# Adding softmax weights of four heads with one VectorE instruction instead of two, in a two-layer attention kernel

## The chip, the cores and the metric

The kernel runs on one core of a Trainium2 chip. The metric is the device time of one execution in microseconds, as the median of some executions. The engines of the core are TensorE (PE in the profile; its weight loads are PEld), VectorE (DVE), ScalarE (ACT), GpSimd (POOL) and SyncE (SP, which here only issues DMAs). Each engine works through its own instructions in order, and semaphores hold an instruction until what it needs is there.

## What is computed

The input is x of shape (4, 256, 64, 64) in fp32: 4 images, 256 channels, 4096 pixels. Two layers follow one another, each with a residual connection and a group normalization (32 groups) ahead of it:

```python
x = x + attention_A(groupnorm(x))   # q: 1x1 convolution; k, v: 2x2 convolution, stride 2; 8 heads of 32
x = x + attention_B(groupnorm(x))   # q, k, v: 1x1; attention in 4 areas; plus a 7x7 depthwise convolution of v; 1x1 projection
# attention: softmax(q k^T / sqrt(32)) v, per head
```

In layer A each of the 4096 queries of an image sees 1024 keys. In layer B the image is cut into 4 areas of 1024 pixels, and a query sees the 1024 keys of its area. So both layers have the same attention work: 4096 queries x 1024 keys x 8 heads an image.

## The kernel before

**Units and steps.** The eight blocks (layer A for four images, then layer B for four images) are cut into units. A unit is one chunk of 512 queries and one half of the heads (4 heads of 32 channels). There are 16 units a block, 128 in all. A unit has 8 steps, one for each tile of 128 keys; so the main loop at the end of `direct_path` makes 1024 steps, numbered by unit g and step j.

**What a step does.** `scores` lets TensorE multiply keys and queries of the four heads (L263); the result is keys by queries, 128x512 for each head, in two PSUM tiles of two heads each. ScalarE takes the exponential of each of the two tiles (L267), a 128x1024 instruction each, and writes the softmax weights p to SBUF. One step later `weighted` multiplies them by the values (L274) and adds up in PSUM over the eight steps. The divisor of the softmax, the sum of p over all keys, is made in two parts: VectorE adds the weights of steps 1 to 7 to those of step 0, element by element (L813, in `sum_up`), and after the last step TensorE multiplies this sum by ones (`divisors`, L283). No maximum is subtracted; the divisors are checked against a limit at the end, and a second program, `general_path`, would run if one were beyond it.

**The tiles p.** The weights of a step lie in two tiles of 128x2x512 fp32 (two heads each) with the tag "p", of which there are 10 buffers. The pair of step 0 is held until the divisors of its unit are made, since the sum is made in it. The chunks of the first image (`first`), one row block at the end (`rb`) and a small tile (`within`) share the tag.

**The order.** The order of instructions on every engine is the order in which the Python code issues them (`manual_schedule`). In each step the code issues the scores, the first exponential, what earlier steps had put off to this one (`later`), the weighted values of the step before, the second exponential, what a plan holds for this step (`plan`, filled by `at(g, j, ...)`), and then parts of side tasks. `soon(n, f)` puts f off by n steps. The additions of a step are put off by one step, the divisors of a unit and what follows them (`divide`) by three.

**What divides.** `divide` copies the divisors out of PSUM (L292), sends them through DRAM so that they lie on 128 partitions (L299, L300, GpSimd's DMA queue), takes reciprocals on VectorE (L306, with a sum for the check in L307), sends them out (L308) and broadcasts them back (L310), and VectorE multiplies the attention result by them (L313). These steps lie in the plan at fixed places of the next two units. Layer A then adds the residual (L436) and takes statistics for the next normalization (L441) on VectorE, and SyncE stores the chunk (L442). Layer B adds the convolution (L573), projects on TensorE (L157, `ops`) and adds bias and residual on VectorE (L588), and SyncE stores the result (L591).

**Side tasks.** Projections to q, k and v, the depthwise convolution as matrix products (L747, with bands and rows that SyncE loads at L728 and L731) and the output projection are side tasks on TensorE. They wait in a queue, `side`, and a step takes none, one, two or three parts of them, by how many wait. All share one PSUM bank (the tag "side"), which must be read out before the next task can write it. The means of the group normalization (L222) need VectorE's aggregate (L217).

Of the kernel before, what the change touches and what calls it, by code (L numbers as in the profile page):

```python
# [9 lines left out]
FP = mybir.dt.float32  # L10
I32 = mybir.dt.int32
AF = mybir.ActivationFunctionType
# [3 lines left out]
P = 128  # L16
B, C, HH, WW = 4, 256, 64, 64
N = HH * WW
CT = C // P
NH, HD = 8, 32  # L20
NAREA = 4
# [3 lines left out]
NKT = MK // P  # L25
CH = 512
NCH = N // CH
# [12 lines left out]
SCALE = HD ** -0.5  # L40
# [15 lines left out]
def direct_path(  # L56
# [19 lines left out]
    V, S, G, T = nc.vector, nc.scalar, nc.gpsimd, nc.tensor  # L76

    const = ctx.enter_context(tc.tile_pool(name="const", bufs=1))
    pool = ctx.enter_context(tc.tile_pool(name="work", bufs=1))
# [25 lines left out]

    first = [pool.tile([P, CT, CH], FP, tag="p", name=f"first_{c}", bufs=10) for c in range(NCH)]
    for c in range(NCH):
        nc.sync.dma_start(first[c], xv[0][:, :, c * CH : (c + 1) * CH])  # L110
    wq0_sb = const.tile([P, CT, C], FP, name="wq0_sb")
# [34 lines left out]
    ones = const.tile([P, HD], FP, name="ones")  # L146
# [12 lines left out]
    def ps_pair(name):  # L159
        return psum.tile([P, 2, CH], FP, tag="s", name=name, bufs=3)  # L160
# [9 lines left out]
    def at(g, j, f):  # L170
        g, j = g + int(j // NKT), int(j % NKT)
        plan.setdefault((g, j), []).append(f)
# [75 lines left out]
    qs, ks, vs, atts, dens, avs = {}, {}, {}, {}, {}, {}  # L248
# [7 lines left out]

    def scores(unit, j):
        q, k = unit[1](), unit[2]()
        p = [pool.tile([P, 2, CH], FP, tag="p", name="p", bufs=10) for _ in range(2)]
        pairs = [ps_pair("s"), ps_pair("s")]  # L260
        for h in range(4):
            rows = slice(HD * h, HD * h + HD)
            T.matmul(  # L263
                pairs[h // 2][:, h % 2, :], lhsT=k[rows, unit[0], j * P : (j + 1) * P], rhs=q[rows, :],
                start=True, stop=True,
            )
        exps = [lambda i=i: S.activation(p[i], pairs[i], AF.Exp, scale=SCALE) for i in range(2)]  # L267
        return p, exps

    def weighted(unit, j, p, av):  # L270

        v = unit[3]()
        for h in range(4):
            T.matmul(  # L274
                av[HD * h : HD * h + HD, :], lhsT=v[:, j, unit[0] * P + HD * h : unit[0] * P + HD * h + HD],
                rhs=p[h // 2][:, h % 2, :], start=(j == 0), stop=(j == NKT - 1),
            )

    def divisors(g, p):

        dens[g] = ps_pair("den")[:, 0, :]
        for h in range(4):
            T.matmul(  # L283
                dens[g][HD * h : HD * h + HD, :], lhsT=ones, rhs=p[h // 2][:, h % 2, :], start=True, stop=True,
            )

    def divide(g, unit):

        den_sb = pool.tile([P, CH], FP, tag="den", name="den_sb", bufs=1)
        few = pool.tile([P, 2, CH // HD], FP, tag="few", name="few", bufs=2)  # L290
        rows = dram.tile([4, CH], FP, tag="rows", name=f"rows_{g}", bufs=4)
        S.copy(den_sb, dens.pop(g))  # L292
        if g == len(units) - 1:
            rb = pool.tile([P, CH], FP, tag="p", name="rb", bufs=10)
            V.reciprocal(rb, den_sb)
            V.tensor_mul(unit[4]()[:, unit[0], :], avs.pop(g), rb)
            spare.extend((den_sb, rb))
            return
        G.dma_start(rows, den_sb[0:P:HD, :])  # L299
        G.dma_start(few[:, 0, :], rows.rearrange("h (q n) -> (h q) n", n=CH // HD))  # L300
        made = {}

        def reciprocals():
            rb = made["rb"] = pool.tile([P, CH], FP, tag="rb", name="rb", bufs=1)
            recs = dram.tile([4, CH], FP, tag="recs", name=f"recs_{g}", bufs=4)
            V.reciprocal(few[:, 1, :], few[:, 0, :])  # L306
            V.tensor_reduce(sums[:, :, g], few, AX.X, ALU.add)  # L307
            G.dma_start(recs.rearrange("h (q n) -> (h q) n", n=CH // HD), few[:, 1, :])  # L308
            for h in range(4):
                G.dma_start(rb[HD * h : HD * h + HD, :], recs[h : h + 1, :].to_broadcast([HD, CH]))  # L310

        def multiply():
            V.tensor_mul(unit[4]()[:, unit[0], :], avs.pop(g), made["rb"])  # L313

        at(g + 1, 7, reciprocals)
        at(g + 2, 4, multiply)
# [459 lines left out]
    units = []  # L776
# [16 lines left out]
    def soon(steps, f):  # L793
        later.setdefault(now[0] + steps, []).append(f)
# [13 lines left out]

    def sum_up(g, j, ps):

        for i in range(2):
            if j:
                soon(1, lambda i=i: V.tensor_add(ps[0][i], ps[0][i], ps[j][i]))  # L813
        if j == NKT - 1:
            soon(3, lambda: divisors(g, ps[0]))
            soon(3, lambda: divide(g, units[g]))
# [3 lines left out]
    while now[0] < last or plan or later or side:  # L820
        g, j = divmod(now[0], NKT)
        if now[0] < last:
            if j == 0:
                ps = {}

            ps[j], exps = scores(units[g], j)
            exps[0]()
        for f in later.pop(now[0], []):
            f()
        if before is not None:  # L830
            weighted(*before)
            if j == 0:
                avs[g - 1] = pool.tile([P, CH], FP, tag="av", name="av_sb", bufs=2)
                S.copy(avs[g - 1], before[3])
# [13 lines left out]
        if now[0] < last:  # L848
            if j == 0:
                av = psum.tile([P, CH], FP, tag="av", name="av", bufs=1)  # L850
            sum_up(g, j, ps)
            before = units[g], j, ps[j], av
        now[0] += 1


    within = pool.tile([P, 2 * len(units)], FP, tag="p", name="within", bufs=10)
    V.tensor_scalar(within, sums.rearrange("p k g -> p (k g)"), LIMIT, None, ALU.is_le)
    least = pool.tile([P, 1], FP, tag="least", name="least", bufs=1)
    V.tensor_reduce(least, within, AX.X, ALU.min)
    ps = ps_pair("count")[0:1, 0, 0:1]  # L860
# [550 lines left out]
def two_attention_layers(tc: tile.TileContext, *args: bass.AP):  # L1411
    nc = tc.nc
    with tc.tile_pool(name="verdict", bufs=1) as pool:
        bad = pool.tile([1, 1], I32, name="bad")
        direct_path(tc, *args, bad)
        count = nc.values_load(
            bad, min_val=0, max_val=P, skip_runtime_bounds_check_because="a count of partitions"
        )
        with tc.If(count > 0):
            general_path(tc, *args)  # L1420
# [39 lines left out]
```

## Time and profile before

| What | Value |
|---|---|
| Median of 3 runs | 3265.79 us (3263.93 to 3267.28) |
| The profiled execution's own time | 3265.73 us |
| Its span, first to last instruction | 3264.0 us |
| TensorE busy (matmul) | 3181.3 us, 97% |
| VectorE busy | 2508.4 us, 77% |
| ScalarE busy | 2524.3 us, 77% |
| GpSimd busy | 493.6 us, 15% |
| Additions L813 on VectorE | 1792, mean 1220 ns |
| Exponentials L267 on ScalarE | 2048, mean 1026 ns |
| Mean granted TensorE clock | 0.989 |

The profile is one execution on the chip. Busy times are unions: where two instructions of one engine overlap, the time counts once. In the table of groups a row gives the source line, the engine, the operation, the tiles written and read, the shape, the count, then the busy time and the mean of one, and last the engine's idle time ahead of these instructions with the one that ended it. The chain that ended last is followed back from the last instruction, at each step to what released it, or to the one before it on its engine. The timeline lists instructions with start, length, engine, line and count; neighbours of one kind are merged into one row, with the time from the start of the first to the end of the last. The ends of matmuls are modelled.

### The profile page before, as it was taken

Reading aid. Unit: us, or ns where it says so; the run is one execution under the profiler, and the core shown is the slowest. Engines: PE = TensorE matmul, PEld = TensorE weight load, DVE = VectorE, ACT = ScalarE, POOL = GpSimd, SP = SyncE. Lnnn points to the kernel's source line nnn. Section 1 sums busy time; section 2 is a strip of 40 time slices with the busy share of each in tenths; the row PEclk is TensorE's granted clock in tenths of the full one; section 3 lists DMA queues with packets and bytes.
Section 4 is the critical chain, followed back from the end, with each engine's and each line's share of the span. In section 5 each row is a group of like instructions: output and inputs, shape, how many; then the busy total and the mean of one; then the engine's idle time right before and its main releaser. Section 6 shows DMA issues by size and latency. Waiting matters only on the chain.

```text
span 3264.0 us, 75650 instructions
## 1 busy us (share of the span) xinstructions
PE 3181.3 (97%) x30754; PEld 963.2 (30%) x30754; DVE 2508.4 (77%) x2717; ACT 2524.3 (77%) x2993; POOL 493.6 (15%) x923
## 2 busy tenths in 40 slices
PE   7999999999999999999999899999999999999997
PEld 4233322233233333223222223232232333222221
DVE  3777896778877777778767577777787788788887
ACT  3888787787887778888867677777777777788775
POOL 0111121111211111111111111111111111111111
PEclk9999999999999999999999999999999999999998
DMA  5243434454444456677766666666554655523212
GB/s 179 44 109 78 109 89 93 96 125 108 114 114 132 122 153 154 173 174 174 187 168 151 164 155 165 174 154 170 135 156 124 156 157 152 135 68 81 65 47 57
DMA packets 648172, 421.50 MB, mean 129 GB/s; under 512 B 411756, under 2 KB 556620, under 8 KB 647816
## 3 DMA queue, kind: packets, MB, share of 16 engines
q1 hardware_dynamic: 619368, 380.11, 46.0%
q0 software_dynamic: 28448, 36.48, 4.6%
q8 instruction: 244, 4.00, 0.5%
q14 instruction: 112, 0.92, 0.1%
HBM read 318.32 MB, written 98.09 MB: 128 GB/s over the span
## 4 chain that ended last, share of the span: by engine, by line
PE 87%; DMA 6%; issue 2%; SPq 2%; DVE 1%; ACT 1%; POOL 0%; DVEq 0%; ACTq 0%; POOLq 0%
PE s L263 31%; PE av L274 27%; PE den L283 4%; DMA rows<-vals 4%; PE ops L157 3%; PE k0ps L157 3%; PE q0ps L157 3%; PE v0ps L157 3%; PE k1ps L157 3%; PE vals_ps L157 3%; PE conv_ps L747 3%; PE q1ps L157 3%; DVE p L813 1%; ACT p L267 1%; SPq L556 1%
## 5 line engine op out<-in xcount | busy, mean ns | idle before, releaser
L813 DVE TENSOR_TENSOR p<-p 128x1024 f32<-128x1024 f32 x1792 | 2111.2, 1220 | 543.6 <-ACT p L267 491.1
L267 ACT ACTIVATE p<-s 128x1024 f32<-128x1024 f32 x2048 | 2016.3, 1026 | 539.0 <-PE s L263 524.3
L263 PE MATMUL s<-q,k_A 32*128 32x512 f32 x4096 | 603.9, 640 | 6.9 <-ACT p L267 6.6
L263 PE MATMUL s<-q,k_B 32*128 32x512 f32 x4096 | 600.1, 646 | 0.3 <-ACT p L267 0.3
L274 PE MATMUL av<-p,v_B 128*32 128x512 f32 x4096 | 550.5, 608 | 0.0
L274 PE MATMUL av<-p,v_A 128*32 128x512 f32 x4096 | 549.7, 604 | 0.0
L310 POOL DMA_DIRECT2D rb<-recs x508 | 252.0, 501 | 451.5 <-DMA recs<-few 367.1
L263 PEld LDWEIGHTS s<-q,k_B 32*128 32x128 f32 x4096 | 166.3, 184 | 386.7 <-issue 297.0
L263 PEld LDWEIGHTS s<-q,k_A 32*128 32x128 f32 x4096 | 173.2, 183 | 338.0 <-issue 253.5
L308 POOL DMA_DIRECT2D recs<-few x127 | 70.0, 551 | 1284.8 <-DVE sums L307 1207.5
L274 PEld LDWEIGHTS av<-p,v_B 128*32 128x32 f32 x4096 | 87.9, 108 | 384.2 <-issue 340.5
L274 PEld LDWEIGHTS av<-p,v_A 128*32 128x32 f32 x4096 | 88.6, 108 | 381.3 <-issue 333.5
L747 PE MATMUL conv_ps<-rows,band 88*32 88x128 f32 x4096 | 139.2, 277 | 28.9 <-DMA rows<-vals 28.9
L747 PEld LDWEIGHTS conv_ps<-rows,band 88*32 88x32 f32 x4096 | 123.8, 139 | 100.6 <-issue 80.3
L157 PE MATMUL ops<-cv,wp_sb 128*32 128x512 f32 x1024 | 136.3, 612 | 9.9 <-issue 6.4
L300 POOL DMA_DIRECT2D few<-rows x127 | 72.3, 569 | 477.5 <-DMA rows<-den_sb 468.0
L283 PE MATMUL den<-p,ones 128*32 128x512 f32 x1024 | 138.7, 604 | 2.2 <-DVE p L813 2.2
L299 POOL DMA_DIRECT2D rows<-den_sb x127 | 74.4, 586 | 436.7 <-ACT den_sb L292 429.9
L157 PE MATMUL k0ps<-taps,wk_sb 128*32 128x256 f32 x2048 | 128.9, 383 | 3.0 <-ACT taps L245 3.0
L157 PE MATMUL q1ps<-h,wqkv_sb 128*32 128x512 f32 x1024 | 131.5, 592 | 0.0
L157 PE MATMUL vals_ps<-hv,wqkv_sb 128*32 128x512 f32 x1024 | 130.2, 594 | 0.0
L157 PE MATMUL k1ps<-h,wqkv_sb 128*32 128x512 f32 x1024 | 128.7, 592 | 0.2 <-ACT cout L758 0.2
(86 smaller groups left out, 1690.8 us busy)
## 6 DMA issues: line engine op xcount, KB each, us to landing
rows<-vals SPq DMA_DIRECT2D x512, 195.9 KB
rb<-recs POOLq DMA_DIRECT2D x508, 64.0 KB, 3.2
band<-mats SPq DMA_DIRECT2D x128, 176.0 KB
vala<-vout SPq DMA_DIRECT2D x128, 144.0 KB
vals<-vout SPq DMA_DIRECT2D x128, 144.0 KB
vc<-vala SPq DMA_DIRECT2D x64, 288.0 KB
hq<-in_x SPq DMA_DIRECT2D x32, 512.0 KB
xc<-in_x SPq DMA_DIRECT2D x32, 512.0 KB
```

Of the source, the lines that this page charges most:

```text
L157: T.matmul(out[cols, :], lhsT=lhsT[:, cols], rhs=rhs, start=start, stop=stop)
L263: T.matmul(pairs[h // 2][:, h % 2, :], lhsT=k[rows, unit[0], j * P : (j + 1) * P], rhs=q[rows, :], start=True, stop=True,)
L267: exps = [lambda i=i: S.activation(p[i], pairs[i], AF.Exp, scale=SCALE) for i in range(2)]
L274: T.matmul(av[HD * h : HD * h + HD, :], lhsT=v[:, j, unit[0] * P + HD * h : unit[0] * P + HD * h + HD], rhs=p[h // 2][:, h % 2, :], start= ...
L283: T.matmul(dens[g][HD * h : HD * h + HD, :], lhsT=ones, rhs=p[h // 2][:, h % 2, :], start=True, stop=True,)
L299: G.dma_start(rows, den_sb[0:P:HD, :])
L300: G.dma_start(few[:, 0, :], rows.rearrange("h (q n) -> (h q) n", n=CH // HD))
L308: G.dma_start(recs.rearrange("h (q n) -> (h q) n", n=CH // HD), few[:, 1, :])
L310: G.dma_start(rb[HD * h : HD * h + HD, :], recs[h : h + 1, :].to_broadcast([HD, CH]))
L556: nc.sync.dma_start(cv[:, t, :].rearrange("p (f r x) -> p r f x", f=TX, r=RC)[:, y - c * RC], conv[b][t * P : (t + 1) * P, r * TX : (r + 1 ...
L747: T.matmul(ps[HD * m : HD * m + HD, (2 * k + i) * size : (2 * k + i + 1) * size].rearrange("p (y x) -> p y x", y=NY), lhsT=band[:, half].r ...
L813: soon(1, lambda i=i: V.tensor_add(ps[0][i], ps[0][i], ps[j][i]))
```

## The change

A step's weights of all four heads lie in one tile of 128x4x512 (128x2048). The tag "p" has 5 buffers of this size instead of 10 of half the size. The two exponentials each write one half of the tile. VectorE adds a step's weights to the sum in one instruction of 128x2048 instead of two of 128x1024, put off by one step as before. The matmuls read the same data from the new tile. The chunks of the first image lie in pairs in such tiles.

```diff
-    first = [pool.tile([P, CT, CH], FP, tag="p", name=f"first_{c}", bufs=10) for c in range(NCH)]
+    first = [pool.tile([P, 2, CT, CH], FP, tag="p", name=f"first_{a}", bufs=5) for a in range(NAREA)]
+    first = [first[c // 2][:, c % 2] for c in range(NCH)]
...
     def scores(unit, j):
         q, k = unit[1](), unit[2]()
-        p = [pool.tile([P, 2, CH], FP, tag="p", name="p", bufs=10) for _ in range(2)]
+        p = pool.tile([P, 4, CH], FP, tag="p", name="p", bufs=5)
...
-        exps = [lambda i=i: S.activation(p[i], pairs[i], AF.Exp, scale=SCALE) for i in range(2)]
+        exps = [lambda i=i: S.activation(p[:, 2 * i : 2 * i + 2], pairs[i], AF.Exp, scale=SCALE) for i in range(2)]
...
-                rhs=p[h // 2][:, h % 2, :], start=(j == 0), stop=(j == NKT - 1),
+                rhs=p[:, h, :], start=(j == 0), stop=(j == NKT - 1),
...
-                dens[g][HD * h : HD * h + HD, :], lhsT=ones, rhs=p[h // 2][:, h % 2, :], start=True, stop=True,
+                dens[g][HD * h : HD * h + HD, :], lhsT=ones, rhs=p[:, h, :], start=True, stop=True,
...
-            rb = pool.tile([P, CH], FP, tag="p", name="rb", bufs=10)
+            rb = pool.tile([P, CH], FP, tag="p", name="rb", bufs=5)
...
     def sum_up(g, j, ps):
 
-        for i in range(2):
-            if j:
-                soon(1, lambda i=i: V.tensor_add(ps[0][i], ps[0][i], ps[j][i]))
+        if j:
+            soon(1, lambda: V.tensor_add(ps[0], ps[0], ps[j]))
...
-    within = pool.tile([P, 2 * len(units)], FP, tag="p", name="within", bufs=10)
+    within = pool.tile([P, 2 * len(units)], FP, tag="p", name="within", bufs=5)
```

## The prediction

> **What bounds the kernel now.** I read the engine shares first, then the chain of work that ended last, then the cost groups of the two lines that the change touches, and then single stretches of the timeline.
>
> ```profile
> span 3264.0 us, 75650 instructions
> PE 3181.3 (97%) x30754; PEld 963.2 (30%) x30754; DVE 2508.4 (77%) x2717; ACT 2524.3 (77%) x2993; POOL 493.6 (15%) x923
> ...
> PE 87%; DMA 6%; issue 2%; SPq 2%; DVE 1%; ACT 1%; POOL 0%; DVEq 0%; ACTq 0%; POOLq 0%
> ...
> L813 DVE TENSOR_TENSOR p<-p 128x1024 f32<-128x1024 f32 x1792 | 2111.2, 1220 | 543.6 <-ACT p L267 491.1
> L267 ACT ACTIVATE p<-s 128x1024 f32<-128x1024 f32 x2048 | 2016.3, 1026 | 539.0 <-PE s L263 524.3
> ```
>
> TensorE is busy 97% of the span and has 87% of the chain; VectorE has 77% and 1%. VectorE's cost is large (2111.2 us in the additions of L813) but lies beside TensorE's work. The last column of the L813 row is the one that matters: VectorE mostly stands idle until ScalarE's exponential (L267) ends, so it runs as soon as it can and is not behind. A step of the main loop takes TensorE 2.93 us with one side task (scores 1.07, weighted values 1.00, side task 0.86, from the chain), and VectorE needs some 2.3 to 2.4 us of it. Only where a step has no side task (2.07 us) does VectorE fall behind, for some steps. TensorE's gaps that end on VectorE are few: 1.25 us at 494, 1.14 at 1444, 0.72 at 3153 and 3197, 1.05 at 3235, 0.13 at 902, 5.0 us in all, without the first 20 us, the last 20 and one at 1801 that a load causes.
>
> [...] So I use the 97% only beside the step times, which repeat at 2.93 us where nothing waits; the trace agrees that TensorE paces.
>
> **Prices.** [...] From the trace alone: 512 elements take 687 ns (L313), 1024 take 1220, so 2048 take 1220 + 2 x 533 = 2286 ns. I take 2286. [...] independent instructions start some 84 ns before the end of the one ahead (a pair takes 2.36 us, not 2.44), but L307, which reads what L306 wrote, starts 34 ns after its end.
>
> **The change part by part.**
>
> 1. Instructions. 1792 additions at 1220 ns become 896 at 2286. Two that overlap take 2.36 us from start to end, so a pair becomes 0.07 us shorter. VectorE's busy time goes from 2508 to about 2508 - 2111 + 896 x 2.286 = 2445 us (75%). TensorE's work hides this; it is worth nothing by itself.
>
> 2. A later start. Before, the first addition of a pair starts when the first exponential of its step ends. The one addition reads all four heads, so it waits for the second, about 0.92 us later. In the 896 pairs of the trace I compared starts: 650 begin before the second exponential ends; of these the usual delay is 0.9 us (1.5 where the second exponential also waits), and the end of the sum is later by 0.9 - 0.07 = 0.83 us (1.06 where the second half had waited itself). For the 246 that start late anyway the end is 0.07 us earlier. Behind the waiting addition on VectorE are reciprocals (L306), divisions (L313), residuals (L436), L573 and L588, all late by the same 0.8 us until an idle gap takes it up. No queue is reordered. GpSimd's queue, which stands 1207 us for L307 in all, issues the reciprocals' DMAs 0.8 later; their broadcast is due at L313 five steps on, and VectorE waited for it 14 times (33 us), mostly where L307 itself is not late. SyncE's queue is rival B.
>
> 3. Adjacent sums. The addition of step j reads the sum of step j-1. Before, the other half lay between; now, where nothing else does, the next sum starts 34 ns after the end: 2286 + 34 = 2320 against 2 x 1140 = 2280, 0.04 us worse. With another instruction between it is 2286 - 84 = 2202, 0.08 us better.
>
> 4. Waits. ScalarE's and TensorE's waits on the tile have the same order; the weighted values of a step come 1 us or more after the second exponential. Ten half tiles become five tiles of the same bytes. A tile comes back after four steps; there the exponential starts 0.74 us after the last use in the tightest case, and over 3 us in 99%. A delay of 0.7 in a backlog just fits: I cost it at nothing. The divisors (L283) wait for a whole sum rather than its first half, but end with the second in both. Each of the 128 has 5.0 us of slack in the median; six have under 0.4.
>
> **Where 0.8 us late reaches TensorE.** It is late work only where a VectorE result is due at once. The clearest is at 2878, on VectorE, then on TensorE:
>
> ```profile
> 2863.26 2.36 DVE L813 TENSOR_TENSOR p<-p 128x1024 f32<-128x1024 f32 x2 [0.81 <-ACT p L267]
> 2865.54 0.68 DVE L313 TENSOR_TENSOR att_B<-av_sb,rb 128x512 f32<-128x512 f32 x1
> 2866.14 2.35 DVE L813 TENSOR_TENSOR p<-p 128x1024 f32<-128x1024 f32 x2
> 2868.41 2.12 DVE L573 SCALAR_TENSOR_TENSOR cv<-cv,bpe_sb,att_B 128x512 f32<-128x512 f32 x2
> 2870.36 4.62 DVE L813 TENSOR_TENSOR p<-p 128x1024 f32<-128x1024 f32 x4
> 2874.88 0.26 DVE L306 RECIPROCAL few<-few 128x16 f32<-128x16 f32 x1
> 2875.18 0.19 DVE L307 TENSOR_REDUCE sums<-few 128x2 f32<-128x32 f32 x1
> 2875.28 2.35 DVE L813 TENSOR_TENSOR p<-p 128x1024 f32<-128x1024 f32 x2
> 2877.55 0.75 DVE L588 SCALAR_TENSOR_TENSOR xm<-ops,bproj_sb,xm 128x512 f32<-128x512 f32 x1
> ```
> ```profile
> 2877.50 1.06 PE L274 MATMUL av<-p,v_B 128*32 128x512 f32 x8
> 2878.38 1.04 PE L157 MATMUL ops<-cv,wp_sb 128*32 128x512 f32 x8
> ```
>
> From 2863.26 on VectorE is never idle. L588 ends at 2878.30 and frees the one side bank of PSUM; the next projection needs it at 2878.38. After: the first sum starts 0.91 later, at the end of the second exponential (2864.14); from there -0.08 at each of the four sums that another instruction follows and +0.04 at the one followed by a sum: 0.91 - 0.32 + 0.04 = 0.63 us. TensorE stands 0.63 - 0.08 = 0.55 us that it did not stand before.
>
> The same pattern stands at 2970, 3062, 3154 and 3197, where L588 is already the last to come: 4 x 0.63. With 2878: 3.1 us. The group means at 495 and 902 are waited for and end such runs (first pair released by L267, three or four sums): 0.6 + 0.7. The divisors at 367 have 0.1 us slack and a run that begins with a second half (1.06 less 5 x 0.08): 0.6. L588 at 2741 has 0.35 slack behind a reciprocal 0.87 late: 0.5. At the end of the program the last sum, its divisors, reciprocal and projection are all in line: 0.65. Sum of losses 3.1 + 1.3 + 0.6 + 0.5 + 0.65 = 6.2 us. Gains: the runs before 456, 1446 and 1493 begin on something other than an exponential and shrink by 0.2 to 0.3, of which TensorE feels some 0.3. Net +5.9.
>
> The profiled execution took 3265.73 us, 1.7 more than its span, and stands 0.06 under the median. 3265.7 + 5.9 gives 3271.6, and with a little for what I did not list **3272**, +0.19%. A measurement of this kernel tells about 0.2% (6.5 us) from no change, so this lies at the edge.
>
> **The rivals.**
>
> A, absorbed (not slower): the late sums are taken up by idle time, as for most of the 896, and the few tight places move, since TensorE's standing gives VectorE time. For it: 5.0 us median slack. Against: the late runs repeat with the same 0.05 us margin. Time 3264 to 3268, say 3266.
>
> B, slower: SyncE's queue is in order and stands for VectorE results: 459 us for L588 (30 times), 208 for L436 (13), 142 for the memset behind L688 (19). A result 0.84 late sends that queue, and the loads of rows and bands behind it, off 0.84 late, and 19 waits of TensorE for rows<-vals (28.9 us) would each grow: 19 x 0.84 = 16 us, 3288 with the losses above, 3280 if half of them do. It decides where the queue's wait for VectorE ends within 0.84 us of the convolution freeing its buffer. Against: that queue stood 358 us for the convolution itself, so it is mostly early. Bound below: the loads could also miss each other and save a few us.
>
> C, faster: the listed gaps of TensorE that end on VectorE sum to 5.0 us, so even without them it is 3261, under 0.2%. It needs luck with the loads.
>
> D, that one addition is done at half rate or split: 2286 would not be seen. Nothing speaks for it.
>
> **How the numbers follow.** Main case 0.55, its own range 3268 to 3276, split evenly by the bound at 3272.3; A 0.20, almost all within; B 0.20, slower; C and D 0.05. Faster 0.05, same 0.46, slower 0.49. Range 3263 to 3282: it takes in A and the half-sized B, and leaves some 0.15 out.
>
> **What would show it.** L813: 896 at some 2286 ns, busy near 2048, its idle time released by L267 nearly always. VectorE near 75%. TensorE's gaps ended by VectorE up from 5 to some 11 us, at L588 late in the run, the group means and the end. Wrong if those gaps do not grow (A), if waits for rows<-vals grow by over 5 us (B), or if the mean of L813 is not 2286 (D).

## The result, and the profile after

The changed kernel takes 3273.73 us in the median of 20 runs (3264.6 to 3279.72). The kernel before, run again beside it, takes 3267.36 us (20 runs, 3259.68 to 3275.7). The ratio is 1.002 with a 95% interval of 1.0013 to 1.0028: it is slower by about 6.4 us, between 4 and 9. Forecast were +6.3 us (3272 from 3265.7). The profiled execution after took 3278.12 us, 4.4 above its median, and the one before 3265.73, 1.6 below the median of all its runs. So the two traces differ by 12.4 us, twice the change. Single numbers from them are good where a place repeats, not as a sum.

The page of the changed kernel (line numbers from L109 to L810 are higher by one than before; the addition is still L813):

```profile
span 3276.4 us, 73360 instructions
...
PE 3182.1 (97%) x30754; PEld 962.2 (29%) x30754; DVE 2444.8 (75%) x1821; ACT 2524.1 (77%) x2993; POOL 498.7 (15%) x923
...
PE 83%; DMA 5%; DVE 4%; issue 3%; ACT 2%; SPq 1%; POOL 0%; DVEq 0%; POOLq 0%; ACTq 0%
...
L813 DVE TENSOR_TENSOR p<-p 128x2048 f32<-128x2048 f32 x896 | 2049.1, 2287 | 672.2 <-ACT p L268 660.0
L268 ACT ACTIVATE p<-s 128x1024 f32<-128x1024 f32 x2048 | 2016.0, 1026 | 543.7 <-PE s L264 536.0
```

VectorE works 64 us less (2508.4 to 2444.8) and the kernel is slower. What VectorE saved is in the last column of L813: it waits 660 us for the exponentials where it waited 491. TensorE's busy time is the same (3181.3, 3182.1); its share of the chain fell from 87 to 83% and VectorE's rose from 1 to 4%. So TensorE has new waits, and they end on VectorE.

The waits of TensorE, engine and line, then what ended the wait, total us, times, longest; first before, then after:

```profile
PE conv_ps L747 <- DMA rows<-vals: 28.9, 19, 7.0
...
PE ops L157 <- DVE xm L588: 3.5, 3, 2.0
...
PE den L283 <- DVE p L813: 2.2, 2, 1.1
...
PE gm_B L222 <- DVE few L306: 1.2, 1, 1.2
```
```profile
PE conv_ps L748 <- DMA rows<-vals: 32.5, 19, 8.2
...
PE den L284 <- DVE p L813: 6.4, 4, 3.0
PE ops L158 <- DVE xm L589: 6.1, 6, 1.6
...
PE gm_B L223 <- DVE few L307: 2.8, 2, 1.9
```

In each kernel one of the waits for xm (2.0 us before, 1.2 after) lies at 1801 to 1807, where VectorE itself waits for a load (xm<-xmid, 5.49 us before, 3.80 after). Without it, and with two short ones that these lines leave out (0.13 us before, at the group mean of 902; 0.40 after, at 2748), the gaps that end on VectorE are 5.0 us before and 14.5 after. The list counts only the idle time ahead of a row of matmuls. Before, the divisors of heads 0 and 1 could start while the sum of heads 2 and 3 was not done, and the wait inside such a row is not in the list; so the 5.0 us are too few, by some 0.6 at each of the divisors of 1444 and 3235 (six matmuls take 1.67 us there, where eight without a wait take 1.06).

The stretch that the prediction worked through, on VectorE and on TensorE, after the change:

```profile
2871.23 2.29 DVE L813 TENSOR_TENSOR p<-p 128x2048 f32<-128x2048 f32 x1 [0.66 <-ACT p L268]
2873.43 0.68 DVE L314 TENSOR_TENSOR att_B<-av_sb,rb 128x512 f32<-128x512 f32 x1
2874.04 2.28 DVE L813 TENSOR_TENSOR p<-p 128x2048 f32<-128x2048 f32 x1
2876.24 2.09 DVE L574 SCALAR_TENSOR_TENSOR cv<-cv,bpe_sb,att_B 128x512 f32<-128x512 f32 x2
2878.18 4.67 DVE L813 TENSOR_TENSOR p<-p 128x2048 f32<-128x2048 f32 x2
2882.76 0.25 DVE L307 RECIPROCAL few<-few 128x16 f32<-128x16 f32 x1
2883.05 0.19 DVE L308 TENSOR_REDUCE sums<-few 128x2 f32<-128x32 f32 x1
2883.15 2.28 DVE L813 TENSOR_TENSOR p<-p 128x2048 f32<-128x2048 f32 x1
2885.35 0.75 DVE L589 SCALAR_TENSOR_TENSOR xm<-ops,bproj_sb,xm 128x512 f32<-128x512 f32 x1
```
```profile
2884.55 1.06 PE L275 MATMUL av<-p,v_B 128*32 128x512 f32 x8
2886.15 1.07 PE L158 MATMUL ops<-cv,wp_sb 128*32 128x512 f32 x8 [0.53 <-DVE xm L589]
```

From the start of the first sum to the start of L589 it is 14.12 us, where it was 14.29. This run of instructions is 0.17 us shorter, but it starts at the second exponential, 0.91 us later against the step. So the read-out of the side bank is late by 0.74 us. The projection starts 1.60 us after the weighted values, where it started 0.88 after them: TensorE lost 0.72 us here.

### The profile page after: what moved, and what is told of

It reads as the page before. It is cut to its first block, busy times and chain, and to the rows that moved or that the text cites. A ratio compares the mean times of both kernels' runs of the same rounds, so it can differ in the third digit from the quotient of the medians.

```text
span 3276.4 us, 73360 instructions
## 1 busy us (share of the span) xinstructions
PE 3182.1 (97%) x30754; PEld 962.2 (29%) x30754; DVE 2444.8 (75%) x1821; ACT 2524.1 (77%) x2993; POOL 498.7 (15%) x923
## 4 chain that ended last, share of the span: by engine, by line
PE 83%; DMA 5%; DVE 4%; issue 3%; ACT 2%; SPq 1%; POOL 0%; DVEq 0%; POOLq 0%; ACTq 0%
PE s L264 29%; PE av L275 26%; PE den L284 4%; PE v0ps L158 3%; PE k0ps L158 3%; PE q1ps L158 3%; PE q0ps L158 3%; PE vals_ps L158 3%; DVE p L813 3%; PE k1ps L158 3%; PE ops L158 3%; PE conv_ps L748 3%; DMA rows<-vals 3%; ACT p L268 1%; DMA recs<-few 0%
## 5 line engine op out<-in xcount | busy, mean ns | idle before, releaser
L813 DVE TENSOR_TENSOR p<-p 128x2048 f32<-128x2048 f32 x896 | 2049.1, 2287 | 672.2 <-ACT p L268 660.0
L748 PE MATMUL conv_ps<-rows,band 88*32 88x128 f32 x4096 | 138.9, 276 | 32.6 <-DMA rows<-vals 32.5
```

The lines of the kernel that those rows point to most:

```text
L748: T.matmul(ps[HD * m : HD * m + HD, (2 * k + i) * size : (2 * k + i + 1) * size].rearrange("p (y x) -> p y x", y=NY), lhsT=band[:, half].r ...
L813: soon(1, lambda: V.tensor_add(ps[0], ps[0], ps[j]))
```

## The experiments

Theory 1: the cost is that the sum waits for the second exponential; what stands behind it on VectorE is late, and TensorE pays at some dozen places where such a result is due at once. The rivals are in the expectations. Ratios are to the kernel before, run in the same series.

**Tile and additions apart (e1).** The tile of four heads and five buffers stay, two additions:

```diff
-            soon(1, lambda: V.tensor_add(ps[0], ps[0], ps[j]))
+            for half in (slice(0, 2), slice(2, 4)):
+                soon(1, lambda half=half: V.tensor_add(ps[0][:, half], ps[0][:, half], ps[j][:, half]))
```

> The one tile of four heads and the five buffers stay; the sum is made by two additions again, first half first. Theory 1 (the cost is that the sum waits for the second exponential of its step, and TensorE then waits at some dozen places): the start of the first addition is as in the kernel before, so 3266 to 3268 us, TensorE's gaps that end on VectorE back near 5 us in sum. Rival (the coarser tile costs: it comes back to the exponential only when all four heads are read and added): as slow as the changed kernel, 3272 to 3275 us.

Measured: ratio 1.0004 (0.9995 to 1.0012), median 3269.45 us beside 3268.69. TensorE's waits:

```profile
PE ops L158 <- DVE xm L589: 2.9, 3, 1.5
...
PE gm_B L223 <- DVE few L307: 1.2, 1, 1.2
PE den L284 <- DVE p L815: 1.1, 1, 1.1
```

These are the waits of the kernel before, but for the one at 1444, which is gone in this execution. The tile costs nothing that shows (0.12% at most); the one addition is the cost.

**Late start alone (e2).** As e1 with `(slice(2, 4), slice(0, 2))`: the half of the second exponential first, so both additions stand behind it.

> The one tile stays; two additions again, but the half of the second exponential is added first, so that both wait for it. Theory 1 (late start): as slow as the changed kernel or a little slower, 3272 to 3276 us, since a pair ends 0.9 us later than before and is 0.07 us longer than one instruction; gaps of TensorE that end on VectorE 12 us or more. Rival (the cost is that sums which follow one another directly must wait for each other's end, and that the divisors wait for a whole sum): both are gone here, so back to 3266 to 3269 us.

Measured: ratio 1.0047 (1.0033 to 1.0061), median 3286.47 us. TensorE's waits:

```profile
PE ops L158 <- DVE xm L589: 7.2, 6, 2.2
PE den L284 <- DVE p L815: 5.9, 3, 3.0
...
PE gm_B L223 <- DVE few L307: 3.1, 2, 2.1
```

There is no long instruction and no sum that follows its own predecessor, and the same waits are there at the same places. So the late start is enough. One half of the rival is not gone here, as the expectation says it is: the divisors of heads 0 and 1 come first, and their half is now added last, so they still wait for a whole sum (3.00 us at the end, in one row of eight matmuls). The read-outs do not depend on this, and there the rival falls. But the time is some 9 us more than that of the changed kernel, where theory 1 expected 0 to 3: the size is a miss. In the steps at 2876, 2968 and 3060 it loses 0.81 to 0.83 us each, the changed kernel 0.74 to 0.76; over a dozen places that explains 1 us.

**Urgent work first, everywhere (e3, e4).** The additions of a step are issued after its planned work and side tasks, one (e3) or two (e4):

```diff
-            soon(1, lambda: V.tensor_add(ps[0], ps[0], ps[j]))
+            at_close(1, lambda: V.tensor_add(ps[0], ps[0], ps[j]))
...
+        for f in closing.pop(now[0], []):
+            f()
         before = None
```

> One addition of four heads as in the changed kernel, but issued at the end of its step, behind the step's planned work and side tasks, so that reciprocals, divisions, residuals and the read-out of the side bank no longer stand behind an addition that waits for an exponential. Theory 1 (late results behind the waiting sum): TensorE's gaps at L588 late in the run and at the group means go[...]: 3262 to 3267 us, at or below the kernel before. Rival (VectorE's total work in the steps without side tasks is what is late, whatever the order): no gain, 3272 to 3275 us. A new wait is possible: an addition behind a read-out that waits for TensorE; then the divisors are late and it is over 3275 us.

> The same order (additions at the end of their step) with two additions of two heads. Issued there, both exponentials are long done, so nothing is left of the difference in the start. Theory 1: one addition (e3) is then as fast as two or faster by up to 1 us, since it saves 0.07 us a step; both 3262 to 3267 us. Rival (one long instruction is slower by itself, by the waits of adjacent sums): two additions faster than one by 3 us or more.

Measured: e3 1.0015 (1.0007 to 1.0023), e4 1.0012 (1.0001 to 1.0024), medians 3273.19 and 3272.2 us beside 3268.69. No gain, so theory 1 failed here and the rival's times came true. The waits of e3 say why:

```profile
PE den L284 <- DVE p L817: 14.6, 9, 3.5
...
PE ops L158 <- DVE xm L589: 2.1, 1, 2.1
```

The waits for the read-out and the group means are gone (what is left of xm is the one that a load causes), and the divisors wait 14.6 us instead of 6.4: the sums have become late. In e4 the list shows only 4.4 us at the divisors, because with two additions much of their wait lies inside the row of matmuls: the step at 457 us takes 5.30 us, where it took 3.03 before, and the list has 1.27 of it. In steps without a side task (2.07 us) VectorE has more work than time (a sum alone takes 2.29 us), and here the change of order in all of them only made the divisors late instead.

**Only the tight steps (e5, e6).** The list TIGHT has 165 of 1024 steps (the expectations say 160), in eleven stretches that lead up to TensorE's gaps. e5 uses two additions in them and one elsewhere, e6 the reverse (`if tight` in place of `if not tight`):

```diff
+        tight = any(lo <= g * NKT + j <= hi for lo, hi in TIGHT)
+        for whole in ([slice(0, 4)] if not tight else [slice(2 * i, 2 * i + 2) for i in range(2)]):
...
+                soon(1, lambda whole=whole: V.tensor_add(ps[0][:, whole], ps[0][:, whole], ps[j][:, whole]))
```

> The changed kernel, with two additions (first half first) only in the 160 of 1024 steps that lead up to the places where TensorE waited for VectorE in its trace; one addition in the other 84%. Theory 1 (a dozen places make the whole cost): 3266 to 3270 us, as the kernel before, and TensorE's gaps that end on VectorE back near 5 us. Rival (a cost spread over all steps: 0.8 us late in 650 steps, by SyncE's queue or by the exponentials' buffers): 3272 to 3275 us.

> The counterpart: one addition only in those 160 steps, two in all others. Theory 1: the whole cost of the change, 3272 to 3276 us, with the gaps at the group means, at L588 late in the run and at the end as in the changed kernel. Rival (spread cost): 3267 to 3270 us.

Measured: e5 1.0006 (0.9995 to 1.0018), e6 1.0018 (1.0009 to 1.0027). TensorE's waits in e5, then in e6:

```profile
PE ops L163 <- DVE xm L594: 4.1, 3, 2.7
...
PE gm_B L228 <- DVE few L312: 1.2, 1, 1.2
PE den L289 <- DVE p L820: 1.1, 1, 1.1
```
```profile
PE ops L163 <- DVE xm L594: 7.1, 6, 2.3
PE den L289 <- DVE p L820: 5.3, 4, 3.0
...
PE gm_B L228 <- DVE few L312: 2.7, 2, 1.9
```

With one addition in a sixth of the steps alone the kernel is as slow as the changed one, and with one addition in the other 84% it is not to be told from the kernel before. The intervals of e5 and e6 overlap, so the times alone do not part them; the steps in the traces do. A step is taken from its first scores to those of the next. The table shows by how many us the profiled execution of each kernel exceeds that of the kernel before, in the steps of TIGHT (with the one behind each stretch) and in all others:

| Kernel | Steps of TIGHT | All other steps |
|---|---|---|
| changed | +10.2 | +1.5 |
| e6, one addition in TIGHT | +8.6 | +7.1 |
| e2, second half first everywhere | +12.7 | +8.5 |
| e8, second half first in TIGHT (below) | +9.4 | +7.1 |
| e1, two additions | -1.6 | -4.0 |
| e5, two additions in TIGHT | +1.5 | +2.1 |

The first column follows the late start: 8.6 to 12.7 us with it, at most 1.5 without. The second varies from execution to execution. Between the kernel before and the changed kernel, five of these other steps differ by over 1.5 us. In one TensorE waits for loads (7.9 us at 1845 before, 9.7 at 1848 after), in one for VectorE that itself waits for a load (2.04 at 1799, 1.19 at 1804), in one for an exponential (nothing at 509, 0.91 at 511). In two it waits for nothing, but its clock is 0.63 of full speed in one execution and 1.00 in the other (4.57 and 2.93 us a step at 2478 and 2486; 2.92 and 4.53 at 1863 and 1869, there with the lower clock after). The spread cost falls.

**Late start in the tight steps only (e8).** Two additions, second half first in TIGHT, first half first elsewhere.

> Two additions everywhere; the half of the second exponential first in the 160 tight steps, the other half first elsewhere. Everywhere-second-half-first gave some 12 us more than the changed kernel, which theory 1 does not explain: its sums end only 0.1 us later. If these 12 us come from the tight places too: 3283 to 3287 us. If they are spread over the other steps: as the changed kernel, 3272 to 3276 us.

Measured: 1.0033 (1.002 to 1.0046), between the two, and its interval touches both, so the times do not decide. In the table the steps of TIGHT cost 9.4 us in e8 and 12.7 in e2, beside 10.2 in the changed kernel: little of the 9 us between the medians of e2 and the changed kernel shows there. In the profiled executions of these two, 7.7 of 9.9 us are a longer busy time of TensorE (3189.8 and 3182.1 us) with the same matmuls. Why e2 costs so much more stays open.

**Urgent work first, in 19 steps (e7, e11, e9, e10).** e7: two additions, and in 19 steps alone they are issued at the end of the step. e11 is e7 again; e9 is the changed kernel with this order; e10 has it with two additions in TIGHT and one elsewhere. The excerpt is from e9; e7 has the two additions of e1 in place of the one.

```diff
+URGENT = {*range(137, 144), *range(265, 272), 896, 928, 960, 992, 1008}
...
+            put = at_close if g * NKT + j + 1 in URGENT else soon
+            put(1, lambda: V.tensor_add(ps[0], ps[0], ps[j]))
```

> Two additions everywhere, issued at the end of their step in 19 steps alone, where a group mean or the read-out of the side bank is due at once, and early as before in all others. In the runs with the additions at the end of every step these places took 0.6 to 1.7 us less than in the kernel before, and the loss was elsewhere, at divisors. Theory 1: 2 to 4 us under the kernel before, 3263 to 3267 us, if nothing new becomes late. Rival (the time lost moves to the next wait): as before, 3267 to 3270 us.

> The changed kernel (one addition of four heads) with only this added: in 19 steps, those where a group mean or the read-out of the side bank is due at once, the addition is issued at the end of its step. Theory 1: of the 12 places where the changed kernel loses, the two group means and the five read-outs go; what is left are divisors at 366, 1421 and 1443 us, the read-out at 2740 and the end, 4 to 5 us. So 1 to 3 us from the kernel before, ratio 0.999 to 1.001. Rival (one long addition costs in itself): as the changed kernel, ratio 1.002.

> Both remedies: two additions in the 160 tight steps, one in all others, and the additions behind the urgent work in the 19 steps. Theory 1: as the two-addition kernel with urgent work first, ratio 0.998 to 0.999; the single additions outside the tight steps neither gain nor lose, since nobody waits for them there. Rival (shorter total VectorE work gains something of its own): ratio under 0.997.

> The kernel with two additions and urgent work first in 19 steps, run again beside the others: 0.9982 of the kernel before in its first series. If that was real: 0.997 to 0.999. If it was the luck of that series: 0.9995 to 1.0005.

Measured: e7 0.9982 (0.9974 to 0.999), again as e11 0.9979 (0.9971 to 0.9987); e9 0.9989 (0.9978 to 0.9999); e10 0.9985 (0.9972 to 0.9998). e7 beats both kernels, by about 0.2% against before and 0.4% against the changed one (from the two ratios). The place that lies at 3153 us in the kernel before, where the last pair of sums stands ahead of the read-out:

```profile
3150.88 2.35 DVE L813 TENSOR_TENSOR p<-p 128x1024 f32<-128x1024 f32 x2
3153.15 0.75 DVE L588 SCALAR_TENSOR_TENSOR xm<-ops,bproj_sb,xm 128x512 f32<-128x512 f32 x1
```
```profile
3153.95 1.07 PE L157 MATMUL ops<-cv,wp_sb 128*32 128x512 f32 x8 [0.72 <-DVE xm L588]
```

The same place in e7, VectorE and then TensorE (its profiled execution is the slowest of its 22, 3274.71 us beside a median of 3267.06; places are read from it, not its time):

```profile
3162.35 0.75 DVE L592 SCALAR_TENSOR_TENSOR xm<-ops,bproj_sb,xm 128x512 f32<-128x512 f32 x1 [0.26 <-PE ops L161]
3163.02 7.09 DVE L823 TENSOR_TENSOR p<-p 128x1024 f32<-128x1024 f32 x6
```
```profile
3163.28 1.06 PE L278 MATMUL av<-p,v_B 128*32 128x512 f32 x8
3164.16 1.04 PE L161 MATMUL ops<-cv,wp_sb 128*32 128x512 f32 x8
```

The read-out (here L592) is now ahead of the last pair of sums and ends at 3163.10. The projection follows the weighted values after 0.88 us, with no wait. The kernel before lost 0.93 us at this step and at the like one at 3195, and 0.9 at the group mean of 492; these are gone, in e11 too. The gain of e7, 5.8 us between the medians, is larger than these 2.8 us and than the 2 to 4 us that were expected; the rest is not explained. e9 shows that the order mends the changed kernel as well; in e10, not to be told from e7 or e9, the single additions outside the tight steps bring no gain that shows.

## Why the prediction was right, point by point

**Prices.** Right. L813 took 2287 ns (2286 taken), its busy time is 2049.1 us (2048), VectorE's 2444.8 (2445).

**Later start.** Right as a mechanism: shown by e1 (gone with two additions), e2 (there without the long instruction) and e5 and e6 (it sits in a sixth of the steps). The places were named: the means at 495 and 902 (gaps 1.25 to 1.95 and 0.13 to 0.85; +0.6 and +0.7 forecast), the divisors at 367 (0.70; 0.6 forecast), L588 at 2741 (0.40; 0.5), the five read-outs.

**Adjacent sums.** Mis-sized. I took 34 ns between the end of a sum and the next that reads it, from L306 and L307. Two such sums take 4.67 us in the stretch above, 4.67 - 2 x 2.287 = 0.10 us apart. That is 0.06 to 0.07 more at each such pair. Also, two halves next to two others had taken 2.26 us, not the 2.28 that I used. So the run became 0.17 us shorter instead of 0.28, and the five late read-outs cost 0.74 to 0.85 us a step, where 0.55 to 0.63 were forecast: 3.9 us instead of 3.1.

**Gains in runs that start on something else.** Right at 456 and 1493, where the steps are 0.11 and 0.20 us shorter. Wrong at 1446, for a reason that the prediction does not have. TensorE there, before and after:

```profile
1445.03 1.67 PE L283 MATMUL den<-p,ones 128*32 128x512 f32 x6 [1.14 <-DVE p L813]
1446.53 0.60 PE L283 MATMUL den<-p,ones 128*32 128x512 f32 x2
1447.91 1.14 PE L263 MATMUL s<-q,k_A 32*128 32x512 f32 x8
```
```profile
1451.80 1.06 PE L284 MATMUL den<-p,ones 128*32 128x512 f32 x8 [2.22 <-DVE p L813]
1454.36 2.07 PE L264 MATMUL s<-q,k_A 32*128 32x512 f32 x8
```

The gap grew by 1.1 us, but it costs next to nothing by itself: before, the divisors of heads 2 and 3 waited too, inside the row. They ended 1.11 us after the sum of these heads, and now all end 1.21 us after the one sum. So "end with the second in both" holds but for 0.1 us. What costs is the clock of TensorE behind the longer gap: the next scores take 2.07 us instead of 1.14, at a clock of 0.50 instead of 1.00. This step and the next are 1.68 us longer. My estimate from the trace is the same: the clock stays at 0.50 for 3.41 us (see the last section), and at half the clock half of that time is lost, 1.7 us. At 1427, which I had not listed, a step lost 0.54 us. The run of VectorE before it starts with a division whose broadcast comes later, since its reciprocal was 0.7 us late: against the step it starts 0.63 us later. It also has three sums in a row, 7.08 us where six halves took 6.89. I had cost late broadcasts at nothing.

**The end.** Forecast were 0.65 us; from the last scores on, the end took 1.4 us longer. The divisors, before and after:

```profile
3236.21 1.67 PE L283 MATMUL den<-p,ones 128*32 128x512 f32 x6 [1.05 <-DVE p L813]
```
```profile
3249.21 1.93 PE L284 MATMUL den<-p,ones 128*32 128x512 f32 x8 [3.05 <-DVE p L813]
```

The last sum ended at 3237.20 before and at 3249.06 after, 7.98 and 8.84 us after the last scores: 0.86 late. The eight matmuls then take 1.93 us, where the same eight took 1.06 at 1451.80: TensorE is at half speed here (a clock of 0.50 from 3248.29 on). So ScalarE's copy of the divisors, at 3238.36 and 3251.20, is 1.84 us later against the last scores, and some 0.45 us of this came back up to the end, which runs partly at half speed in both kernels (0.50 from 3243.24 us on before, for 6.83 us, and from 3248.29 on after, for 13.65). What the prediction put at nothing is the clock.

**The sum.** Forecast were losses of 6.2 us and gains of 0.3. In the two profiled executions the steps at the listed places lost 8.1 us and gained 0.3 at 456 and 1493; 1427 and 1446 add 2.2, of which the clock has some 1.7. That makes 10.0 us, and the medians differ by 6.4, between 4 and 9. The profiled execution after lies 4.4 us above its median, so its sum need not be the usual one. The places and the cause were right; that the total met the medians more closely than the terms met the traces is in part luck, for the adjacent sums and the end were too small and the clock was left out.

**The rivals.** A, absorbed: wrong, the interval lies clear of 1. B, SyncE's queue and the loads: that queue's waits for L588 grew as feared (459.2 to 477.5 us, 30 times), but TensorE's waits for rows<-vals grew by 3.6 us only (28.9 to 32.5), under the 5 us named as the sign of B. Single profiles show 37.6 (e7) and 26.7 (e9), so this figure varies from execution to execution and decides nothing alone; e5, which has 84% of the late sums, costs nothing that shows. C and D: not seen.

## What to carry to other kernels

Two instructions that start as their inputs come can beat one that waits for the last input, even on an engine with a quarter of its time free, if results behind it in the same queue are due at once: here 1.0004 of the kernel before with two additions (e1) and 1.002 with one. Count the places where the bound engine waits for that engine, and look at what stands ahead of the late result in its queue: here moving the additions behind urgent work in 19 of 1024 steps gave 0.2%, and moving them behind it everywhere gave nothing. The same merge cost nothing that shows in the steps where nobody was waiting (e5, 1.0006, with one addition in 84% of the steps).

## What was not expected of the hardware

Some gaps of TensorE were followed by a stretch at half its clock and so went with a loss beyond their length, 1.68 us behind the one at 1446. In the tables of windows below, the figure after POOL's is the clock granted to TensorE as a share of full speed. First the changed kernel, behind the gap of 2.22 us that ends at 1451.80 and around the one of 1.95 us that ends at 497.47:

```profile
1452.90:1456.20 3.30, 3.30 (x16) 0.52 (x8) 2.69 (x2) 1.51 (x2) 1.41 (x3) 0.50 0.07 21
493.00:499.00 6.00, 4.05 (x42) 1.71 (x42) 5.97 (x9) 3.96 (x6) 0.55 (x1) 1.00 0.67 140
499.00:505.00 6.00, 6.00 (x60) 1.85 (x56) 3.53 (x5) 4.78 (x6) 2.23 (x5) 1.00 0.62 140
```

Then the kernel before, around the gap of 1.14 us that ends at 1445.03 and behind one of 1.69 us that ends at 2112.27:

```profile
1443.00:1449.00 6.00, 4.86 (x35) 0.95 (x31) 5.97 (x8) 3.66 (x5) 0.55 (x1) 1.00 0.43 84
1449.00:1455.00 6.00, 6.00 (x104) 3.00 (x104) 3.83 (x4) 5.91 (x8) 2.56 (x5) 1.00 0.47 118
2113.50:2116.80 3.30, 3.30 (x20) 0.60 (x16) 1.35 (x4) 2.18 (x3) 0.00 (x0) 0.50 0.84 212
```

After the gap of 2.22 us TensorE runs at half speed (0.50) for 3.41 us, and so it does after that of 1.69, and even after one of 0.91 us that ends at 513.33 in the changed kernel (0.50 from 514.22 on); after those of 1.14 and 1.95 it stays at full speed (1.00). The length of the gap alone does not decide. The clock records of these two executions have 22 stretches at half speed that end within the span: 14 of 3.41 us, two of 6.83, five of 10.24 and one of 13.65, so each is 3.41 us or a multiple of it. The gap at 1446 grew from 1.14 to 2.22 us, and such a stretch stands only behind the longer one; what decides was not shown. Whether stretches that come in one execution and not in another are part of the spread of 15 us between the runs of one kernel was not tested.
